# Content scores added to the positional scores tile by tile, and one product with the values

## The chip, the cores and the metric

The kernel runs on one core of one Trainium2 chip. The metric is device time in microseconds (us) of one execution; a figure for a kernel is the median of several executions.

## The reference, cut to what matters

Two layers work on an input of 4 images with 16 x 16 pixels and 1024 channels. Layer 0 is a convolution-like attention (a "lambda" layer), layer 1 is a causal attention with a mixture of eight experts behind it. Only layer 0 is touched. After a group norm it computes:

```
q = bn(x @ Wq);  k = x @ Wk;  v = bn(x @ Wv)       # 4 heads of q, one k, one v
q = q.reshape(b, heads, dim_v, m)                  # m = 256 pixels, dim 256
k = softmax(k.reshape(b, 1, dim_v, m), axis=-1)
v = v.reshape(b, 1, dim_v, m)
Lc = einsum('bukm,buvm->bkv', k, v)                # content
Yc = einsum('bhkn,bkv->bnhv', q, Lc)
rel = rel_pos_emb[rel_pos[..., 0], rel_pos[..., 1]]
Lp = einsum('nmku,buvm->bnkv', rel, v)             # position
Yp = einsum('bhkn,bnkv->bnhv', q, Lp)
x = x + (Yc + Yp).reshape(b, hh, ww, heads * dim_v)
```

Both terms end in a sum over m of a score with v: the content score is the sum over k of q and the softmax of k, the positional score is the sum over k of q and rel. The two kernels differ in whether the two scores are summed before the product with v. The reshapes are plain reinterpretations of memory, so a row of the matrix k after the reshape is made of pixels that lie 4 apart in x.

## The kernel before

Everything is float32. TensorE (PE) multiplies a stationary operand of up to 128 x 128 (loaded by LDWEIGHTS) with a moving operand of up to 512 columns; the results land in PSUM banks of 128 x 512. One pool of PSUM tiles has three banks tagged `mm` and three tagged `tr`, used in turn. A scheduler orders the instructions of each engine when the program is built; each engine then works through its own list strictly in order, and waits on semaphores. `small`, `l0`, `proj`, `tpool` and so on are pools in the on-chip memory SBUF. `big` has two places of 32 KB per partition, and `wpool` two of 16 KB; a new tile in such a place waits for the last use of the old one.

Layer 0 goes through these stages:

1. **Group norm and q.** `xn` (place `big0`) holds the normed input, channels on partitions. Products `pq` (L265) give q; VectorE (DVE) scales and shifts it (L269, L273) into `q0`, laid out [k within a half, half, pixel row i, pixel column j, batch and head]. The last index has 16 values, `BH`: four batches with four heads.
2. **k.** For each of eight tiles `t` (two for each batch) `pk` (L311) is a product over 8 chunks of channels with 256 result columns. VectorE takes the row maximum (L315), ScalarE (ACT) the exponential (L318), VectorE divides (L320). Two transposes `pkt` (L323) on TensorE and a copy (L324) put the result into `k_T`.
3. **v.** Four products `pv` (L334) and ScalarE's copies make `v_T`, pixels of m on partitions.
4. **Position.** In four rounds over `R` (in the order 1, 2, 0, 3), with 16, 15, 8 and 7 pixel rows `n_i`, GpSimd (POOL) copies a window of the embedding (L384), 32 products `pT` (L386) multiply it with q0, and ScalarE and VectorE take turns to copy the PSUM bank into `T` (L394). `T` is a tile of pool `tpool`, which has two of them. Then SyncE (SP) issues one or two transfers for each pixel row (L401), from `T` to its shifted place in `s0`, the positional scores [m within a half, half, i, j, BH] in place `big0`. R = 0 writes only upper pixel rows (ni from 8 on) of the first half of m; R = 3 writes only rows below 8, of the second half of m; R = 1 and R = 2 write both.
5. **Content.** `content()` is called before R = 3: four pairs of products `pl` (L355) of k_T and v_T make `lc` (ScalarE's copy, L362), which is Lc of the reference.
6. **First loop over the tiles.** For each of eight token tiles (batch b, half nt of the pixel rows) `pyc` (L414) multiplies q0 with lc; VectorE adds the result to `xs[t]`, the residual x (L421).
7. **Second loop.** For each tile `pyp` (L434) multiplies s0 with v_T; VectorE adds it to xs[t] (L441); `layer_norm` takes statistics (L159, L161), ScalarE normalises (L166), TensorE transposes (L170), ScalarE copies into `ln1` (L171) in place `big1`, where q0 was. GpSimd adds a bias to xs[t] (L443) and SP stores the row tile (L444).

After that `project_v` (products at L482) begins layer 1. It reads ln1, the first half of the tokens (tiles 0 to 3) first. Attention and the experts follow; they are the same in both kernels.

Of the kernel before, what the change touches and what calls it, by code (L numbers as in the profile page):

```python
# [30 lines left out]
F32 = mybir.dt.float32  # L31
I32 = mybir.dt.int32
AF = mybir.ActivationFunctionType
ALU = mybir.AluOpType
# [3 lines left out]
P = 128  # L38
C = 1024
NC = C // P  # L40
B = 4
M = 256
TOK = B * M
NT = TOK // P
HEADS0 = 4
BH = B * HEADS0
SIDE = 16
# [6 lines left out]
HALF = 512  # L54
# [9 lines left out]
def kernel(  # L64
# [27 lines left out]
    nc = tc.nc  # L92
# [13 lines left out]
    def big_tile(n, name, shape=(NC, TOK)):  # L106
        return big[n].tile([P, *shape], F32, tag="big", name=name)
# [11 lines left out]
    def mm(name):  # L119
        return ps.tile([P, HALF], F32, tag="mm", name=name)  # L120

    def tr(name):
        return ps.tile([P, HALF], F32, tag="tr", name=name)
# [7 lines left out]
    ident = const.tile([P, P], F32, tag="ident", name="ident")  # L131
# [7 lines left out]
    xs = tiles_of_x("x")  # L139
# [34 lines left out]
    with ExitStack() as layer0:  # L174
        l0 = pool(layer0, "l0")
        xn = big_tile(0, "xn")
# [8 lines left out]
            nc.gpsimd.dma_start(vp[:, i, :], a)  # L185
        emb = l0.tile([P, 2, REL, REL], F32, tag="emb", name="emb")
        v_T = l0.tile([P, 2, TOK], F32, tag="v_T", name="v_T")
        lc = l0.tile([P, B, 2, M], F32, tag="lc", name="lc")

        q0 = big_tile(1, "q0", (2, SIDE, SIDE, BH))  # L190

        with ExitStack() as projection:
            proj, projw = pool(projection, "proj"), pool(projection, "projw", 2)
# [5 lines left out]
            first_root = small.tile([P, 1], F32, tag="first_root", name="first_root", bufs=1)  # L199
            nc.scalar.activation(first_root, ident[:, 0:1], AF.Sqrt)  # L200

            q_scale = proj.tile([P, C], F32, tag="q_scale", name="q_scale")
            q_shift = proj.tile([P, C], F32, tag="q_shift", name="q_shift")
            bn = proj.tile([P, 2, C], F32, tag="bn", name="bn")
            mean_q, var_q = bn[:, 0, :], bn[:, 1, :]
            for t, a in ((q_scale, q_gamma), (q_shift, q_beta), (mean_q, q_mean), (var_q, q_var)):
                nc.sync.dma_start(t, a.partition_broadcast(P))
            nc.sync.dma_start(emb.rearrange("p c i j -> p c (i j)"), embT)
# [95 lines left out]
            w_kv = w_tile("w_kv", Wk, Wv)  # L304


            k_T = l0.tile([P, 2, B, 4, 64], F32, tag="k_T", name="k_T")
            for t in range(NT):
                pk = mm(f"pk{t}")
                for c in range(NC):  # L310
                    nc.tensor.matmul(  # L311
                        pk[:, :M], xn[:, c, ts(t, P)], w_kv[:, c, :M], start=(c == 0), stop=(c == NC - 1)
                    )
                top = small.tile([P, 1], F32, tag="k_top", name=f"k_top{t}")
                nc.vector.tensor_reduce(top, pk[:, :M], AX.X, ALU.max, negate=True)  # L315
                k_e = projw.tile([P, M], F32, tag="k_e", name=f"k_e{t}")
                total = small.tile([P, 1], F32, tag="k_total", name=f"k_total{t}")
                nc.scalar.activation(k_e, pk[:, :M], AF.Exp, bias=top, accum_out=total)  # L318
                nc.vector.reciprocal(total, total)
                nc.vector.tensor_scalar(k_e, k_e, total, None, ALU.mult)  # L320
                pt = tr(f"pkt{t}")
                for j in range(2):
                    nc.tensor.transpose(pt[:, ts(j, P)], k_e[:, ts(j, P)], ident)  # L323
                nc.vector.tensor_copy(  # L324
                    k_T[:, :, t // 2, :, ts(t % 2, 32)],
                    pt[:, : 2 * P].rearrange("p (j d k) -> p j k d", j=2, k=4),
                )


            for j in range(2):  # L330
                for th in range(2):
                    pv = mm(f"pv{j}_{th}")
                    for c in range(NC):
# [4 lines left out]
                            start=(c == 0),  # L338
                            stop=(c == NC - 1),
# [6 lines left out]
                        scale=vp[:, 0, j : j + 1],  # L346
                    )


        def content():  # L350
            for b in range(B):
                pl = mm(f"pl{b}")
                for kc in range(2):
                    for j in range(2):
                        nc.tensor.matmul(  # L355
                            pl[:, ts(kc, M)],
                            k_T[:, j, b, 2 * kc : 2 * kc + 2, :].rearrange("p k d -> p (k d)"),
                            v_T[:, j, ts(b, M)],
                            start=(j == 0),
                            stop=(j == 1),  # L360
                        )
                nc.scalar.copy(lc[:, b, :, :].rearrange("p k v -> p (k v)"), pl)  # L362

# [1 line left out]
        S2 = SIDE // 2  # L367
        s0 = big_tile(0, "s0", (2, SIDE, SIDE, BH))
        tpool = pool(layer0, "tpool", 2)
        for R, first, n_i in ((1, 0, 16), (2, 0, 15), (0, 8, 8), (3, 0, 7)):  # L370
            if R == 3:
                content()
            rows = min(S2, REL - S2 * R)
            parts = rows * SIDE
            group = 2 if n_i > S2 else 4
            T = tpool.tile([P, n_i, SIDE, BH], F32, tag="T", name=f"T{R}", padded_shape=[P, SIDE, SIDE, BH])
            for n0 in range(0, SIDE, group):
                pT = mm(f"pT{R}_{n0}")
                out_T = pT[:parts, : group * BH * n_i].rearrange("p (j i h) -> p j i h", j=group, h=BH)
                for g in range(group):  # L380
                    nj = n0 + g
                    at = SIDE - 1 - nj
                    window = tpool.tile([P, 2, rows, SIDE], F32, tag="window", name=f"window{R}_{nj}", bufs=4, padded_shape=[P, 2, S2, SIDE])
                    nc.gpsimd.tensor_copy(window, emb[:, :, S2 * R : S2 * R + rows, at : at + SIDE])  # L384
                    for kc in range(2):
                        nc.tensor.matmul(  # L386
                            out_T[:, g, :, :],
                            window[:, kc, :, :].rearrange("p i j -> p (i j)"),
                            q0[:, kc, first : first + n_i, nj, :],
                            start=(kc == 0),  # L390
                            stop=(kc == 1),
                        )
                evict = nc.scalar.copy if n0 // group % 2 == 0 else nc.vector.tensor_copy
                evict(T[:parts, :, n0 : n0 + group, :].rearrange("p i j h -> p j i h"), out_T)  # L394
            for i in range(n_i):
                ni = first + i
                start = S2 * R + ni - SIDE + 1
                for mh in range(2):
                    lo, hi = max(start, mh * S2), min(start + rows, mh * S2 + S2)
                    if lo < hi:  # L400
                        nc.sync.dma_start(  # L401
                            s0[(lo - mh * S2) * SIDE : (hi - mh * S2) * SIDE, mh, ni, :, :],
                            T[(lo - start) * SIDE : (hi - start) * SIDE, i, :, :],
                        )


        for t in range(NT):
            b, nt = divmod(t, 2)
            for hp in range(2):
                py = mm(f"pyc{t}_{hp}")  # L410
                for hl in range(2):
                    bh = b * HEADS0 + 2 * hp + hl
                    for kc in range(2):
                        nc.tensor.matmul(  # L414
                            py[:, ts(hl, M)],
                            q0[:, kc, ts(nt, S2), :, bh].rearrange("p i j -> p (i j)"),
                            lc[:, b, kc, :],
                            start=(kc == 0),
                            stop=(kc == 1),
                        )  # L420
                nc.vector.tensor_add(xs[t][:, ts(hp, HALF)], xs[t][:, ts(hp, HALF)], py)  # L421

        ln1 = big_tile(1, "ln1")
        ln_rows = wpool.tile([P, 4, C], F32, tag="w", name="ln_rows")
        bp = ln_rows[:, 3, :]
        nc.gpsimd.dma_start(bp, b_proj.partition_broadcast(P))
        for t in range(NT):
            b, nt = divmod(t, 2)
            for hp in range(2):
                py = mm(f"pyp{t}_{hp}")  # L430
                for hl in range(2):
                    bh = b * HEADS0 + 2 * hp + hl
                    for mh in range(2):
                        nc.tensor.matmul(  # L434
                            py[:, ts(hl, M)],
                            s0[:, mh, ts(nt, S2), :, bh].rearrange("p i j -> p (i j)"),
                            v_T[:, mh, ts(b, M)],
                            start=(mh == 0),
                            stop=(mh == 1),
                        )  # L440
                nc.vector.tensor_add(xs[t][:, ts(hp, HALF)], xs[t][:, ts(hp, HALF)], py)  # L441
            layer_norm(ln_rows[:, t % 3, :], t, ln1)
            nc.gpsimd.tensor_add(xs[t], xs[t], bp)  # L443
            nc.sync.dma_start(x_rows[ts(t, P), :], xs[t])  # L444
    x_home.close()
# [788 lines left out]
```

## Time and profile before

| | us |
|---|---|
| median of 3 runs | 1333.54 (1332.22 to 1333.65) |
| the profiled execution | 1332.32 |
| its span, first to last instruction | 1330.5 |
| TensorE busy in the span | 1289.7 |
| VectorE busy | 664.7 |
| GpSimd busy | 348.9 |
| ScalarE busy | 247.6 |
| mean granted TensorE clock | 0.992 of full speed |

The times in all views count from the first instruction. PE stands for matmuls, PEld for LDWEIGHTS, which overlap them. One float32 matmul instruction appears as two rows. A timeline line gives the start, the length, the engine, the line of the code, the operation, output<-input, the shape and the count; a bracket tells how long the engine was idle before it and what ended that. "SPq" are transfers that SyncE issues. A line of stretches gives its borders, its length, the busy time of PE, PEld, DVE, ACT and POOL, and then the granted clock, the share of the DMA engines and GB/s. The part of the trace that the change touches runs from about 129 us (`pk`) to 302 us (the first `project_v`).

### The profile page before, as it was taken

How to read it: one execution, taken by the hardware profiler on the slowest of the kernel's cores; microseconds unless marked ns; L12 is line 12 of the kernel's file. 1: busy time of each engine (PE TensorE's matmuls, PEld its weight loads, DVE VectorE, ACT ScalarE, POOL GpSimd, SP SyncE). 2: the span in 40 equal slices, each digit the busy share in tenths (PEclk: the TensorE clock that was granted, in tenths of full speed). 3: DMA queues.
4: the chain of work that ended last, by engine and by line, in shares of the span. 5: the costliest groups of instructions: out<-in, count | busy, mean ns of one | idle time of the engine just before them, and what ended most of it. 6: DMA issues, size and time to landing. Idle time of an engine off the chain costs nothing. (4 is left out here: it accounts for less than half of the span.)

```text
span 1330.5 us, 12205 instructions
## 1 busy us (share of the span) xinstructions
PE 1289.7 (97%) x4492; PEld 710.3 (53%) x4492; DVE 664.7 (50%) x1255; ACT 247.6 (19%) x577; POOL 348.9 (26%) x370
## 2 busy tenths in 40 slices
PE   6999999999999999999999998999999999999994
PEld 3444759998884555555554544444444444444442
DVE  5664301377232555554444756664645555554641
ACT  3200111041000333333323322111101111011110
POOL 0000015042000111112111113545444535445520
PEclk9999999999999999999999999999999999999997
DMA  9210013113102202010505215375666557474532
GB/s 355 117 64 16 0 64 95 34 80 112 64 1 64 64 0 64 1 64 1 190 15 194 95 64 204 91 210 132 184 162 155 160 140 203 101 233 93 114 62 33
DMA packets 60944, 136.11 MB, mean 102 GB/s; under 512 B 5936, under 2 KB 20288, under 8 KB 60880
## 3 DMA queue, kind: packets, MB, share of 16 engines
q1 hardware_dynamic: 47232, 93.27, 20.2%
q0 software_dynamic: 13648, 42.01, 14.5%
q8 instruction: 37, 0.61, 0.2%
q14 instruction: 27, 0.22, 0.1%
HBM read 97.51 MB, written 33.55 MB: 99 GB/s over the span
## 5 line engine op out<-in xcount | busy, mean ns | idle before, releaser
L708 POOL DMA_INDIRECT w_e_xg<-rows,gather x156 | 163.4, 1047 | 69.1 <-issue 44.5
L1078 PE MATMUL p<-w_e,A 128*128 128x512 f32 x384 | 171.8, 597 | 1.8 <-DVE slot L945 1.8
L598 POOL TENSOR_TENSOR s<-s,total 128x256 f32<-128x256 f32 x64 | 51.5, 826 | 341.2 <-DVE total L595 341.2
L1078 PEld LDWEIGHTS p<-w_e,A 128*128 128x128 f32 x384 | 73.5, 191 | 94.1 <-issue 92.4
L639 PE MATMUL po<-w_p,y_T 128*128 128x512 f32 x256 | 116.1, 598 | 0.0
L736 POOL DMA_INDIRECT out_dram<-y,add x32 | 58.6, 1832 | 214.3 <-ACT y L1084 146.5
L1078 PE MATMUL p<-T,S 128*128 128x512 f32 x256 | 112.7, 592 | 0.0
L1084 ACT ACTIVATE y<-y,slot 128x512 f32<-128x512 f32 x64 | 46.2, 722 | 340.1 <-DVE y L1092 166.8
L265 PE MATMUL pq<-w_q,xn 128*128 128x512 f32 x224 | 101.0, 603 | 1.6 <-ACT xn L244 1.6
L729 PE MATMUL one_pe<-w_e,one 128*128 128x512 f32 x224 | 97.3, 592 | 0.0
L482 PE MATMUL pqk<-ln,w_qk 128*128 128x512 f32 x192 | 85.0, 592 | 0.0
L1078 PEld LDWEIGHTS p<-T,S 128*128 128x128 f32 x256 | 48.6, 190 | 60.8 <-issue 60.7
L639 PEld LDWEIGHTS po<-w_p,y_T 128*128 128x128 f32 x256 | 46.3, 190 | 49.1 <-issue 48.7
L729 PEld LDWEIGHTS one_pe<-w_e,one 128*128 128x128 f32 x224 | 42.6, 190 | 53.6 <-issue 53.6
L265 PEld LDWEIGHTS pq<-w_q,xn 128*128 128x128 f32 x224 | 42.5, 193 | 51.8 <-issue 48.6
L588 ACT ACTIVATE s<-s,top 128x256 f32<-128x256 f32 (+1 forms) x128 | 56.6, 443 | 17.4 <-DVE top L586 17.3
L482 PEld LDWEIGHTS pqk<-ln,w_qk 128*128 128x128 f32 x192 | 35.9, 190 | 42.1 <-issue 41.1
L718 DVE STREAM_TRANSPOSE A<-w_e_xg 128x1024 f32<-128x1024 f32 x32 | 39.7, 1240 | 36.1 <-DMA w_e_xg<-rows,gather 36.1
L482 PE MATMUL pqk<-T,S_qk 128*128 128x512 f32 x128 | 57.7, 593 | 0.0
L1078 PE MATMUL p<-w_e,S 128*128 128x512 f32 x128 | 57.5, 592 | 0.0
L1078 PE MATMUL p<-T,A 128*128 128x512 f32 x128 | 57.5, 592 | 0.0
L611 ACT COPY s_T<-pst 128x384 f32<-128x384 f32 x64 | 27.5, 481 | 158.3 <-PE pst L610 158.3
(251 smaller groups left out, 1791.5 us busy)
## 6 DMA issues: line engine op xcount, KB each, us to landing
w_e<-in_expert_w_dram SPq DMA_DIRECT2D x16, 2048.0 KB
w_qk<-in_W_attnT_dram SPq DMA_DIRECT2D x8, 1024.0 KB
xn<-in_xT_dram SPq DMA_DIRECT2D x8, 512.0 KB
x<-in_x_dram SPq DMA_DIRECT2D x8, 512.0 KB
w_v<-in_W_attnT_dram SPq DMA_DIRECT2D x2, 2048.0 KB
x_rows<-x SPq DMA_DIRECT2D x8, 512.0 KB
w_p<-in_W_projT_dram SPq DMA_DIRECT2D x2, 2048.0 KB
xb<-x_rows SPq DMA_DIRECT2D x8, 512.0 KB
```

What stands on the lines that cost most here:

```text
L265: nc.tensor.matmul(pq, xn[:, c, ts(t, P)], w_q[kc][:, c, :], start=(c == 0), stop=(c == NC - 1))
L482: nc.tensor.matmul(bank, stationary(c), moving(c), start=(c == 0), stop=(c == NC // 2 - 1))
L588: nc.scalar.activation(s[:, h, cols], s[:, h, cols], AF.Exp, bias=top[:, qt, h : h + 1], accum_out=total[:, qt, h : h + 1],)
L598: nc.gpsimd.tensor_mul(s[:, :, cols], s[:, :, cols], total[:, qt, :].unsqueeze(2).to_broadcast([P, 2, (qt + 1) * P]),)
L611: nc.scalar.copy(s_T[:, h, :], pt[:, : 3 * P])
L639: nc.tensor.matmul(po, y_T[:, c, ts(t, P)], w_p[j][:, c, :], start=(c == 0), stop=(c == NC - 1))
L708: nc.gpsimd.indirect_dma_start(out=row[:, g, :], out_offset=None, in_=table[: (TOK - P) * Q, :] if e == 0 else table, in_offset=bass.Indir ...
L718: nc.vector.transpose(row_T.rearrange("p c (g j) -> p g c j", g=Q), row.rearrange("p g (c i) -> p g c i", c=NC),)
L729: nc.tensor.matmul(pe, row_T[:, c, :], w[j][:, c, :], start=(c == 0), stop=(c == NC - 1))
L736: nc.gpsimd.indirect_dma_start(out=out[: TOK - P, :] if e == 0 else out, out_offset=bass.IndirectOffsetOnAxis(ap=add[:, e, k : k + 1], axi ...
L1078: nc.tensor.matmul(bank, a[:, c, :], b[:, c, :], start=(c == 0), stop=(c == NC // 2 - 1))
L1084: nc.scalar.mul(y[i][:, ts(j, HALF)], y[i][:, ts(j, HALF)], slot[:, e, 1, 2 * pair + i : 2 * pair + i + 1])
```

## The change

The content scores are computed as scores, not through Lc, and added into s0 before the product with v. It has these parts:

- **k.** `k_q` takes the place of `k_T`: [k row within a half, batch, half, m]. `pk` is computed in two halves of 64 result rows for each chunk; the stationary operand is every fourth token of one batch. The softmax result goes straight into k_q; `pkt`, its copy and `k_T` go.
- **Content.** `content(b, ih)` is now called for each tile. For each half `mh` of m it multiplies k_q with q0 (two matmuls of 512 columns: 128 pixels of one half, 4 heads) and VectorE adds the bank into s0. `lc`, `pl`, the `lc` copies, and the first loop with `pyc` and its additions go.
- **Second loop.** The order of the tiles is all batches with the upper pixel rows (nt = 1), then all with the lower ones. content of the next tile is called ahead of the product `py` (before: `pyp`) of the present one.
- **Places.** q0 moves to pool `l0`; `q_scale`, `q_shift` and the batch norm rows move into a tile `q_rows` in place `big1`. The two T buffers become two halves of one tile `two_T`, also in `big1`, used in turn. `tpool` keeps only the windows. `ln1` takes its place in `big1` after two_T.

The diff, cut to its core:

```diff
-        lc = l0.tile([P, B, 2, M], F32, tag="lc", name="lc")
-        q0 = big_tile(1, "q0", (2, SIDE, SIDE, BH))
+        q0 = l0.tile([P, 2, SIDE, SIDE, BH], F32, tag="q0", name="q0")
...
-            q_scale = proj.tile([P, C], F32, tag="q_scale", name="q_scale")
...
+            q_rows = big_tile(1, "q_rows", (NC, TOK))
+            q_scale, q_shift, mean_q, var_q = (q_rows[:, i, :] for i in range(4))
...
-            k_T = l0.tile([P, 2, B, 4, 64], F32, tag="k_T", name="k_T")
+            k_q = l0.tile([P, B, 2, M], F32, tag="k_q", name="k_q")
             for t in range(NT):
+                b, kc = divmod(t, 2)
                 pk = mm(f"pk{t}")
                 for c in range(NC):
-                    nc.tensor.matmul(
-                        pk[:, :M], xn[:, c, ts(t, P)], w_kv[:, c, :M], start=(c == 0), stop=(c == NC - 1)
-                    )
+                    for kl in range(2):
+                        nc.tensor.matmul(
+                            pk[kl * 64 : kl * 64 + 64, :M],
+                            xn[:, c, ts(b, M)].rearrange("p (d r) -> p r d", r=4)[:, 2 * kc + kl, :],
+                            w_kv[:, c, :M],
+                            start=(c == 0),
+                            stop=(c == NC - 1),
+                        )
...
-                nc.vector.tensor_scalar(k_e, k_e, total, None, ALU.mult)
-                pt = tr(f"pkt{t}")
-                for j in range(2):
-                    nc.tensor.transpose(pt[:, ts(j, P)], k_e[:, ts(j, P)], ident)
-                nc.vector.tensor_copy(
...
+                nc.vector.tensor_scalar(k_q[:, b, kc, :], k_e, total, None, ALU.mult)
...
+        def content(b, ih):
+            heads = slice(b * HEADS0, b * HEADS0 + HEADS0)
+            for mh in range(2):
+                pc = (tr if mh else mm)(f"pc{ih}_{b}_{mh}")
                 for kc in range(2):
...
+                    nc.tensor.matmul(
+                        pc,
+                        k_q[:, b, kc, ts(mh, P)],
+                        q0[:, kc, ts(ih, S2), :, heads].rearrange("p i j h -> p (i j) h"),
+                        start=(kc == 0),
+                        stop=(kc == 1),
+                    )
+                to = s0[:, mh, ts(ih, S2), :, heads].rearrange("p i j h -> p (i j) h")
+                nc.vector.tensor_add(to, to, pc.rearrange("p (n h) -> p n h", h=HEADS0))
...
-        for R, first, n_i in ((1, 0, 16), (2, 0, 15), (0, 8, 8), (3, 0, 7)):
-            if R == 3:
-                content()
+        two_T = big_tile(1, "two_T", (2, SIDE, SIDE, BH))
+        for n, (R, first, n_i) in enumerate(((1, 0, 16), (2, 0, 15), (0, 8, 8), (3, 0, 7))):
...
-            T = tpool.tile([P, n_i, SIDE, BH], F32, tag="T", name=f"T{R}", padded_shape=[P, SIDE, SIDE, BH])
+            T = two_T[:, n % 2, :n_i, :, :]
...
-        for t in range(NT):
-            b, nt = divmod(t, 2)
-            for hp in range(2):
-                py = mm(f"pyc{t}_{hp}")
...
-                nc.vector.tensor_add(xs[t][:, ts(hp, HALF)], xs[t][:, ts(hp, HALF)], py)
...
-        for t in range(NT):
-            b, nt = divmod(t, 2)
+        tiles = [(b, nt) for nt in (1, 0) for b in range(B)]
+        for i, (b, nt) in enumerate(tiles):
+            if i == 0:
+                content(b, nt)
+            if i + 1 < NT:
+                content(*tiles[i + 1])
+            t = 2 * b + nt
...
-            layer_norm(ln_rows[:, t % 3, :], t, ln1)
+            layer_norm(ln_rows[:, i % 3, :], t, ln1)
```

More of the change, by code (lines that the diff above doesn't have):

```diff
@@ L200 @@
             nc.scalar.activation(first_root, ident[:, 0:1], AF.Sqrt)
-            q_scale = proj.tile([P, C], F32, tag="q_scale", name="q_scale")
-            q_shift = proj.tile([P, C], F32, tag="q_shift", name="q_shift")
-            bn = proj.tile([P, 2, C], F32, tag="bn", name="bn")
-            mean_q, var_q = bn[:, 0, :], bn[:, 1, :]
+            q_rows = big_tile(1, "q_rows", (NC, TOK))
+            q_scale, q_shift, mean_q, var_q = (q_rows[:, i, :] for i in range(4))
             for t, a in ((q_scale, q_gamma), (q_shift, q_beta), (mean_q, q_mean), (var_q, q_var)):
@@ L319 @@
                 nc.vector.reciprocal(total, total)
-                nc.vector.tensor_scalar(k_e, k_e, total, None, ALU.mult)
-                pt = tr(f"pkt{t}")
-                for j in range(2):
-                    nc.tensor.transpose(pt[:, ts(j, P)], k_e[:, ts(j, P)], ident)
-                nc.vector.tensor_copy(
-                    k_T[:, :, t // 2, :, ts(t % 2, 32)],
-                    pt[:, : 2 * P].rearrange("p (j d k) -> p j k d", j=2, k=4),
-                )
+                nc.vector.tensor_scalar(k_q[:, b, kc, :], k_e, total, None, ALU.mult)
             for j in range(2):
@@ L347 @@
                     )
-        def content():
-            for b in range(B):
-                pl = mm(f"pl{b}")
+        def content(b, ih):
+            heads = slice(b * HEADS0, b * HEADS0 + HEADS0)
+            for mh in range(2):
+                pc = (tr if mh else mm)(f"pc{ih}_{b}_{mh}")
                 for kc in range(2):
[L354 to L362, printed above, removed]
+                    nc.tensor.matmul(
[7 more added lines that the diff above has]
+                nc.vector.tensor_add(to, to, pc.rearrange("p (n h) -> p n h", h=HEADS0))
         S2 = SIDE // 2
@@ L404 @@
                         )
-        for t in range(NT):
-            b, nt = divmod(t, 2)
-            for hp in range(2):
-                py = mm(f"pyc{t}_{hp}")
[L411 to L421, printed above, removed]
         ln1 = big_tile(1, "ln1")
@@ L426 @@
         nc.gpsimd.dma_start(bp, b_proj.partition_broadcast(P))
-        for t in range(NT):
-            b, nt = divmod(t, 2)
+        tiles = [(b, nt) for nt in (1, 0) for b in range(B)]
[5 more added lines that the diff above has]
+            t = 2 * b + nt
             for hp in range(2):
-                py = mm(f"pyp{t}_{hp}")
+                py = mm(f"py{t}_{hp}")
                 for hl in range(2):
```

## The prediction

> **What bounds the kernel.** I read the page's busy times first, then the groups by line of the first 400 us, then the timeline of the stretch that the change touches.
>
> ```profile
> PE 1289.7 (97%) x4492; PEld 710.3 (53%) x4492; DVE 664.7 (50%) x1255; ACT 247.6 (19%) x577; POOL 348.9 (26%) x370
> ```
>
> TensorE has work in 97% of the span, so a microsecond counts if it leaves TensorE's queue, or makes that queue wait. The groups (busy us, mean ns; a float32 matmul shows as two rows, called passes here):
>
> ```profile
> L334 PE MATMUL pv<-xn,w_kv 128*128 128x512 f32 x64 | 27.8, 592 | 0.0
> L311 PE MATMUL pk<-w_kv,xn 128*128 128x256 f32 x128 | 28.9, 379 | 0.0
> L311 PEld LDWEIGHTS pk<-w_kv,xn 128*128 128x128 f32 x128 | 23.8, 190 | 3.4 <-issue 0.5
> L323 PE MATMUL pkt<-ident,k_e 128*128 128x128 f32 x16 | 3.3, 288 | 0.3
> L355 PE MATMUL pl<-v_T,k_T 128*128 128x256 f32 x32 | 7.1, 379 | 0.0
> L414 PE MATMUL pyc<-lc,q 128*128 128x256 f32 x128 | 28.8, 387 | 0.0
> L414 PEld LDWEIGHTS pyc<-lc,q 128*128 128x128 f32 x128 | 28.5, 307 | 0.0
> L421 DVE TENSOR_TENSOR x<-x,pyc 128x512 f32<-128x512 f32 x16 | 11.0, 687 | 17.7 <-PE pyc L414 17.7
> ```
>
> Busy time over count is the pace: 27.8/64 = 0.434 us for a pass of 512 columns, 0.226 for 256. Passes overlap, so means are longer than paces. The last column is idle time of the engine before the group: VectorE waits for TensorE here, not the reverse. Around the scores:
>
> ```profile
> 202.31 40.14 SPq L401 DMA_DIRECT2D s<-T  x60
> 219.25 1.20 ACT L394 COPY T<-pT 128x512 f32<-128x512 f32 x2 [5.80 <-DMA s<-T]
> 219.98 2.02 PE L386 MATMUL pT<-q,window 128*128 128x128 f32 x16 [0.15 <-POOL window L384]
> 221.84 7.07 PE L355 MATMUL pl<-v_T,k_T 128*128 128x256 f32 x32
> 228.75 4.88 PE L386 MATMUL pT<-q,window 128*112 128x112 f32 x48
> 234.34 0.97 ACT L394 COPY T<-pT 112x448 f32<-112x448 f32 x2 [4.80 <-DMA s<-T]
> 235.01 1.80 PE L386 MATMUL pT<-q,window 128*112 128x112 f32 x16 [1.38 <-ACT T L394]
> ```
>
> The second pacemaker is SP: 60 transfers from T to s0 go out one by one, 40.14/60 = 0.669 us each: 23 for R=1, 22 for R=2, 8 for R=0, 7 for R=3 (counted from the loop). Copies into a reused T buffer wait for them (bracket: 5.80 and 4.80 us); TensorE shows only 1.38 us of it, because `pl` and three free PSUM banks cover the rest.
>
> **What the Trainium skill says.** (1) "TensorE: Matmul & The Clock Gate", section "Part 3: Packing small matmuls": results that go to different column groups are computed at the same time. The trace agrees, on attention values with halves of 64 columns:
>
> ```profile
> 507.56 0.87 PE L620 MATMUL pa<-s_T,v 128*64 128x256 f32 x8
> 508.36 0.92 PE L566 MATMUL sc<-qk 64*128 64x256 f32 x8
> ```
>
> Eight passes, four of 256 and four of 128 columns, would take 4 x 0.226 + 4 x 0.113 = 1.36 us in a row; the next group starts after 0.80. (2) "SBUF — State Buffer", section "Door 1: The DMA port swizzle", on 16-byte lines: at least two accesses per line are needed for full rate. The trace agrees on weight loads: `pyc` loads every sixteenth float in 28.5/128 = 0.223 us, 1.74 ns per column, where the mean of a dense load is 190 ns and of this one 307. A moving operand in 16-byte pieces is not in this trace. (3) The first page again, "Part 1: The HAM clock gate": a window of about 3.4 us with TensorE mostly idle is followed by half clock. The trace agrees:
>
> ```profile
> 806.90 1.07 PE L809 MATMUL row_pt<-ident,row 128*128 128x128 f32 x8 [3.68 <-DVE row L827]
> 808.00:812.00 4.00, 3.90 (x22) 1.47 (x23) 3.04 (x12) 0.37 (x1) 0.00 (x0) 0.57 1.05 409
> ```
>
> After a wait of 3.68 us the clock (third number from the end) is 0.57; the wait of 1.38 us at 235 did no such thing.
>
> **Part by part.** Times are on the clock of the trace before until the sum.
>
> *k stage.* The transposes `pkt` go: -3.3 us. The `pk` matmuls double to 128 instructions with 64 result rows each; by (1) a pair runs in the time of one, so 28.9 us stays. Their weights are every fourth float, one per 16-byte line: 64 x 1.74 ns = 0.111 us, free if the two halves load together, and 0.223 per pair against 0.216 to 0.226 of streaming if not: 0 to +1, I take +0.6. Net -2.7. The copies to k_T (3.4 us) leave VectorE, which idles for TensorE there (7.9 before `pk`'s reduction): nothing.
>
> *Content.* `pl` goes: -7.1; `pyc` goes: -28.8. Instead 32 matmuls with 512 columns, 64 passes, moving q0 in pieces of four floats. Four accesses per line should keep the full pace: 64 x 0.434 = 27.8. Bounds: 27.8, and 64 x 512 x 1.74 ns = 57.0 if each float cost what it costs in a strided load; a gain below 27.8 is excluded, dense 512-column passes being no quicker. I take 27.8.
>
> *T halves.* T is now one region in big1, and a copy waits only for transfers that read the pixel rows it overwrites. The copy of R=0 (8 rows) waits for the first 8 of R=1's 23 transfers: 219.25 - 15 x 0.669 = 209.2, before its matmuls end. TensorE's 0.15 goes, and R=0 ends at 221.7. R=3's first three groups follow at once: 226.6. The fourth needs the bank of the first, whose copy (7 rows) waits for 14 of R=2's 22 transfers: 234.34 - 8 x 0.669 = 229.0, plus 0.49 of copy: 229.5. So with `pl` gone TensorE stands 2.9 us instead of 1.4. Fourth group: 231.3.
>
> *First tiles.* Content of the first two tiles, 16 passes, takes 6.9: 238.2. Then `py` of the first waits for two adds into s0, and the second of these for R=0's eight transfers, which follow R=2's: 234.34 + 8 x 0.669 = 239.7, plus 0.69 for the add (from L421's row): 240.4. TensorE stands 2.2 us. Queued behind that add on VectorE are the adds of the second tile, needed later. R=3's seven land at about 244.4; the lower rows and the first write of ln1 over two_T need them only some 10 us and more after 240.
>
> *Second loop.* Before, it ran from `pyp`'s start at 265.24 to `project_v` at 301.90, 36.7 us. It now also holds 48 passes of content, 20.8 us. On VectorE each tile gets two adds of 0.69 in place of L421's; with some 7.9 us per tile for about 5.1 us of its work they fit, yet they stand in one queue with the layer norm. In the built order a tile's transposes come about as much TensorE work after its last product as its norm takes, so small waits appear: I add 0.5 (bounds 0 and 8 x 0.7 = 5.6, one add late per tile). One more set of transposes falls behind the loop's end, which changes its place and not the sum. So 240.4 + 36.7 + 20.8 + 0.5 = 298.4 against 301.9: -3.5.
>
> *Costed at nothing.* ScalarE loses four `lc` copies (2.3 us), waits for TensorE. The windows take freed space and can start after the last q0 add near 133; needed at 187. q0, q_scale and the rest change address only. The eight x_rows stores keep their number on SP, behind the same POOL adds; the rows return after 690. If that cover went, half a microsecond each.
>
> *Clock.* Two waits of 2.9 and 2.2 us, 9 us apart, lie between 1.38 (no throttle) and 3.68 (throttle). Half clock for 3.4 us loses 1.7; the first loss falls into the second wait. For the second +0.6 (bounds 0 and 1.7).
>
> **Sum.** -2.7 - 3.5 + 0.6 = -5.6 us. The profiled execution took 1332.32 (span 1330.5 and 1.8 around it), so 1326.7 for it; it lies 1.2 below the median of the three runs shown, so the median goes to **1327.9**. A check by work alone: 3.3 + 7.1 + 28.8 - 27.8 - 0.6 = 10.8 us leave TensorE, and 3.6 + 0.5 + 0.6 come back as waits and clock: -6.1.
>
> **Rivals.**
> *Slow moving operand (8%).* If pieces of 16 bytes stream as badly as single floats load, a pass takes 512 x 1.74 ns = 0.89 us. That is 64 x 0.457 = 29.2 more, of which 2.2 fall into the wait for R=0: 1354.9, slower. For it: the strided loads' 307 ns. Against: four accesses per line, where the loads have one. It decides from x = (5.6 + 2.2)/64 = 0.12 us more per pass, a pace of 0.556.
> *Halves in a row (4%).* If `pk`'s halves do not overlap, 128 pairs cost 0.216 more each, 27.6: 1355.5. Against: the `pa` rows.
> *VectorE sets the tile's pace (14%).* A norm held up by 0.7 us per tile, eight times, in place of my 0.5: +5.1, 1333.0, no change. For it: VectorE works two thirds of the time there. Against: L421 idled for TensorE.
> *T is still released whole (3%).* Then R=3's copy stays at 234.34, content ends at 235.0 + 1.8 + 6.9 = 243.7 and `py` starts there: +3.3, 1331.2. Against: the waits of the built program.
>
> **From cases to numbers.** My forecast has 69%, and 2% are for what I have not seen: the forecast's own range, from the unknown load, clock and norm costs, is 1323.5 to 1331. With the 17% of the two milder rivals at 1331 to 1333.5, 1323.5 to 1333.5 leaves out somewhat under 2 in 10. A change of 0.2%, 2.7 us, is about what a measurement of this kernel can tell from none. Faster by more: 0.71, nearly all of the forecast (0.66) and a part of the milder rivals (0.05); within: 0.15; slower: 0.14, the two slow cases and the unseen.
>
> **What would show it.** Right: `pk` near 29 us with 256 passes, `pkt`, `pl`, `pyc` gone; content at 0.43 per pass; one TensorE wait of 2 to 3 us before R=3's last group, one before the first `py`; `project_v` about 6 us earlier. Wrong: content passes over 0.5, `pk` at 56, LDWEIGHTS of `pk` over 0.2, waits before the transposes of each tile, clock below 0.9 after 225.

## The result, and the profile after

The changed kernel takes 1327.37 us (median of 6 executions, 1326.66 to 1329.55) against 1333.6 of the kernel before in the same comparison (1332.22 to 1336.36). The ratio is 0.9955, with a 95% interval from 0.9943 to 0.9968: 6.0 us faster, where 5.6 was forecast. The profiled execution of the changed kernel is the slowest of its six: 1329.55, with a span of 1327.7.

First the busy times, from the head of the page:

```profile
PE 1281.9 (97%) x4508; PEld 691.1 (52%) x4508; DVE 659.8 (50%) x1247; ACT 245.4 (18%) x573; POOL 348.1 (26%) x370
```

TensorE's busy time fell by 7.8 us, and its share of the span is the same. The groups of the first 400 us (busy us, mean ns, idle time before) show what was exchanged for what:

```profile
L310 PE MATMUL pk<-w_kv,xn 128*64 128x256 f32 x256 | 27.9, 380 | 0.0
L310 PEld LDWEIGHTS pk<-w_kv,xn 128*64 128x64 f32 x256 | 25.5, 193 | 2.8 <-issue 0.8
L351 PE MATMUL pc<-q,k_q 128*128 128x512 f32 x64 | 29.6, 593 | 0.0
L420 PE MATMUL py<-v_T,s 128*128 128x256 f32 x128 | 31.8, 400 | 3.0 <-DMA s<-two_T 3.0
L359 DVE TENSOR_TENSOR s<-s,pc 128x512 f32<-128x512 f32 x16 | 10.8, 684 | 18.7 <-PE pc L351 13.9 <-DMA s<-two_T 4.9
L170 PE MATMUL ln_pt<-ident,ln_rows 128*128 128x128 f32 x64 | 8.5, 276 | 1.4 <-ACT ln_rows L166 1.4
```

The rows `pkt`, `pl` and `pyc` are gone. `pk` has twice the passes in 27.9 us. A pass of content starts every 0.43 us; the 29.6 is larger than 64 x 0.43 because the passes are spread over many short groups, and the last pass of each counts with its full 0.59 us. The last row has one wait only: the transposes of seven tiles found their input ready, those of the last tile waited 1.4 us.

The timeline around the scores (start, length, engine, and in brackets the idle time ahead with what ended it):

```profile
211.91 28.72 SPq L397 DMA_DIRECT2D s<-two_T  x43
226.48 0.97 ACT L390 COPY two_T<-pT 112x448 f32<-112x448 f32 x2 [8.37 <-DMA s<-two_T]
227.15 1.80 PE L382 MATMUL pT<-q,window 128*112 128x112 f32 x16 [3.21 <-ACT two_T L390]
228.79 7.04 PE L351 MATMUL pc<-q,k_q 128*128 128x512 f32 x16
238.03 1.88 DVE L359 TENSOR_TENSOR s<-s,pc 128x512 f32<-128x512 f32 x3 [4.86 <-DMA s<-two_T]
238.82 5.46 PE L420 MATMUL py<-v_T,s 128*128 128x256 f32 x16 [2.99 <-DMA s<-two_T]
```

Both forecast waits are there. The copies of R=3 start at 226.48, when the fourteenth transfer of R=2 has landed; TensorE stood 3.21 us for the bank that they free. Then `py` stood 2.99 us, for the add at 238.03, which stood for the transfers of R=0. `py` took 5.46 us for 16 passes in place of some 3.7. The clock says why (third number from the end, in stretches of 4 us):

```profile
234.00:238.00 4.00, 1.83 (x5) 0.52 (x3) 0.00 (x0) 0.00 (x0) 0.00 (x0) 1.00 0.52 151
238.00:242.00 4.00, 3.18 (x8) 2.56 (x9) 1.88 (x3) 0.00 (x0) 0.00 (x0) 0.61 0.33 87
242.00:246.00 4.00, 4.00 (x15) 3.05 (x14) 2.97 (x5) 0.00 (x0) 0.00 (x0) 0.96 0.00 0
```

After the second wait TensorE ran at half clock for about 3.4 us, which lost up to 1.7.

### The profile page after: what moved, and what is told of

It is laid out like the page before. It is cut to its first block, busy times and chain, and to the rows that moved or that the text cites. A ratio compares the mean times of both kernels' runs of the same rounds, so it can differ in the third digit from the quotient of the medians.

```text
span 1327.7 us, 12229 instructions
## 1 busy us (share of the span) xinstructions
PE 1281.9 (97%) x4508; PEld 691.1 (52%) x4508; DVE 659.8 (50%) x1247; ACT 245.4 (18%) x573; POOL 348.1 (26%) x370
## 5 line engine op out<-in xcount | busy, mean ns | idle before, releaser
L715 PEld LDWEIGHTS one_pe<-w_e,one 128*128 128x128 f32 x224 | 42.6, 190 | 53.5 <-issue 53.3
```

Of the source, the lines that this page charges most:

```text
L715: nc.tensor.matmul(pe, row_T[:, c, :], w[j][:, c, :], start=(c == 0), stop=(c == NC - 1))
```

## The experiments

Unless another base is named, each is an edit of the changed kernel. Ratios are to the kernel before, run on the same chip; 0.001 is 1.33 us.

### Two queues for the transfers

```
-evict = nc.scalar.copy if n0 // group % 2 == 0 else nc.vector.tensor_copy
+evict = nc.vector.tensor_copy
-nc.sync.dma_start(
+(nc.scalar if i % 2 else nc.sync).dma_start(
```

> The changed kernel, but the transfers from two_T to s0 go out in turn from SP's queue and from ScalarE's, 30 each, and VectorE makes all the copies into two_T, so that ScalarE's queue holds only transfers there. Theory (the pace of one issuing queue sets both waits of TensorE): the transfers end near 200 + 30 x 0.64 = 219 us instead of 240, the waits of 3.21 us before R=3's last group and of 2.99 us before the first py go, and with them the half clock after the second, worth up to 1.7: -6.2 to -7.9 on 1327.4, so 1319.5 to 1321.2. Rival 1 (the transfers themselves are slow, not their issue): both waits stay, 1327.4. Rival 2 (TensorE's next wait takes over: the 12 more copies on VectorE, or the layer norm's transposes): a part of the gain only, 1323 to 1326.

1321.93 us, ratio 0.9909 (0.9893 to 0.9924): some 5.4 to 6.1 below the changed kernel (by medians, by ratios), a little less than the 6.2 to 7.9 expected. The timeline of this run:

```profile
200.28 28.41 ACTq L397 DMA_DIRECT2D s<-two_T  x28
200.31 28.72 SPq L397 DMA_DIRECT2D s<-two_T  x32
225.75 7.04 PE L351 MATMUL pc<-q,k_q 128*128 128x512 f32 x16
232.63 3.72 PE L420 MATMUL py<-v_T,s 128*128 128x256 f32 x16
```

No bracket is left on TensorE's lines, and the 16 passes of `py` take 3.72 us: no wait, no half clock. Issue on one queue set both waits. In the changed kernel's trace each transfer holds SP for 0.59 us, the next follows at 0.64, and a transfer lands about 2 us after its issue, so that three are under way at once: what goes one by one is the issue. Whether SP itself takes the 0.59 us or is held by the queue behind it, the trace does not tell. Two numbers of the expectation were wrong: the transfers end at 229, not 219, and the queues issue 28 and 32, not 30 each. Each queue needs about 0.65 us for a transfer, but both now run dry between the rounds of R and wait for the next copies. The pacemaker has moved to TensorE. This is the fastest kernel of the study.

### Its control: only VectorE copies

The first of the two edits above alone.

> The changed kernel with all copies into two_T on VectorE and the transfers still on SP alone: the control for two_queues, which makes both edits. Theory (issue on one queue is what two_queues mended): both waits of TensorE stay, 1327.4, within 0.8. Rival (ScalarE's copies were the trouble): 1321 to 1323 as in two_queues.

1328.25 us, ratio 0.9965 (0.9952 to 0.9978). Both waits stay:

```profile
227.94 3.17 PE L382 MATMUL pT<-q,window 128*112 128x112 f32 x16 [3.10 <-DVE two_T L390]
238.77 3.91 PE L420 MATMUL py<-v_T,s 128*128 128x256 f32 x16 [0.78 <-DMA s<-two_T]
```

The time is 0.9 above the changed kernel, a little outside the 0.8 expected; no gain came from the copies. The second wait is short here because the half clock came after the first wait: the group of R=3 took 3.17 us in place of 1.80, time that TensorE would otherwise have stood. In most of the runs below half clock came behind the first wait too, and in pk_dense, more_vector and lower_first it lasted 6.8 us there. So 3.4 us of half clock cost up to 1.7 when they fall after the second wait, and next to nothing when they fall before it.

### The same two edits in the kernel before

> The kernel before, with the transfers from T to s0 going out in turn from SP's queue and from ScalarE's, and all copies into T on VectorE: the same edit as in two_queues. Theory (the kernel before loses only 1.4 us to SP's pace, since pl's products and free banks cover the rest): its waits of 1.38 and 0.15 us go, ratio to the kernel before 0.9988, and two_queues, with the work of the change and no wait for transfers in either, then lies the full 10.8 us of removed TensorE work below it. Rival (SP's pace costs the kernel before as much as the changed one): ratio 0.995 and a distance of only 5 to 6 us.

1332.99 us, ratio 0.9993 (0.9983 to 1.0004), no difference that can be told. Its waits of 1.38 and 0.15 us went, but another came, because `lc`'s copies on ScalarE now stand in a queue with transfers:

```profile
227.43 1.99 PE L355 MATMUL pl<-v_T,k_T 128*128 128x256 f32 x8 [0.85 <-ACT lc L362]
```

The distance to two_queues is 0.0084, or 11.2 us, which the two intervals leave open by some 2.5 either way: the removed TensorE work in full (by work alone the prediction had 10.8). With transfers on one queue the distance is 6.0, so about half of the removed work came back as waits and half clock.

### Halves of two_T given back whole

```
 T = two_T[:, n % 2, :n_i, :, :]
+if n > 1:
+    last = two_T[:, n % 2, 17 - n, 0, :]
+    nc.scalar.copy(last[:, 0:1], ident[:, 0:1])
+    nc.vector.tensor_copy(last[:, 1:2], ident[:, 0:1])
```

> The changed kernel, but the halves of two_T are given back whole: ahead of the copies of R=0 and R=3, ScalarE and VectorE each write one float per partition into the last pixel row of the half (not read afterwards), which the last transfer of the older R reads. Theory (row-wise release is part of the gain): R=3's last group waits for all 22 transfers of R=2 instead of 14, 8 x 0.64 = 5.1 us later, 232.3; content then ends at 241.2 and py starts there instead of at 238.8: +2.4, and up to +1.7 more if the longer wait brings half clock for longer: 1329.8 to 1331.5. Rival (only the wait for R=0's transfers before py counts, R=3's wait is inside it): no change, 1327.4.

1326.39 us, ratio 0.9953 (0.9938 to 0.9967): no change. For R=3 this tested nothing: in the built order the two writes stand behind three of the four copies. For R=0 the copies did wait for the last transfer of R=1:

```profile
216.40 0.19 ACT L375 COPY two_T<-ident 128x1 f32<-128x1 f32 x1 [6.29 <-DMA s<-two_T]
217.46 6.74 PE L386 MATMUL pT<-q,window 128*128 128x128 f32 x64 [0.97 <-ACT two_T L394]
226.21 2.06 PE L386 MATMUL pT<-q,window 128*112 128x112 f32 x16 [2.00 <-ACT two_T L394]
```

The new wait of 0.97 us before R=0's matmuls is repaid at once: R=3's last group waits 2.00 instead of 3.21 and starts 42.44 us after the first `pT`, exactly as in the changed kernel (42.43). SP's pace sets that start, and what TensorE does in between doesn't move it. (Here and below the first `pT` is the start of its first weight load, 0.4 us ahead of its first pass.)

### The same, forced by position

```
-T = two_T[:, n % 2, :n_i, :, :]
+T = two_T[:, n % 2, n // 2 * 8 : n // 2 * 8 + n_i, :, :]
```

> The changed kernel, with R=0 in pixel rows 8 to 15 of its half of two_T and R=3 in rows 8 to 14, in place of the first rows, so that their copies wait for the last transfer of the older R: all 23 of R=1, all 22 of R=2. (The run t_whole did not force that for R=3: three of the four copies were placed ahead of the write that waits.) In the built order of this kernel three pairs of content's passes stand ahead of R=3's last group. Theory (whole release is made up by products that need no copy): R=3's copy ends near 232.2, its group 1.6 us later, ten passes of content fill the time to 238.1, and py waits for R=0's transfers as in the changed kernel: 1327.4, within 0.8. Rival (the prediction's fourth rival: the wait comes on top): +2.4 to +3.3, 1329.8 to 1330.7.

1327.5 us, ratio 0.9964 (0.9953 to 0.9976). TensorE:

```profile
223.97 2.75 PE L351 MATMUL pc<-q,k_q 128*128 128x512 f32 x6
231.97 3.30 PE L382 MATMUL pT<-q,window 128*112 128x112 f32 x16 [5.25 <-ACT two_T L390]
235.06 4.52 PE L351 MATMUL pc<-q,k_q 128*128 128x512 f32 x10
239.42 3.71 PE L420 MATMUL py<-v_T,s 128*128 128x256 f32 x16
```

The wait for all 22 transfers is 5.25 us, but six passes of content went ahead of it, the other ten fill the time behind it, and `py` starts 55.1 us after the first `pT`, against 54.1. The prediction's fourth rival took 3.3 us for whole release; it costs 0 to 1.2. Releasing T by rows was not where the gain came from.

### Lower pixel rows first

```
-tiles = [(b, nt) for nt in (1, 0) for b in range(B)]
+tiles = [(b, nt) for nt in (0, 1) for b in range(B)]
```

> The changed kernel with the lower pixel rows (nt=0) of all batches first, then the upper ones. Theory: the first tile then needs R=3's seven transfers, the last of 60: issued at 240.0, landed near 242.5, the add done near 243.3, py there instead of at 238.8: +4.5, with up to +1.7 for half clock: 1331.9 to 1333.6. Rival (the order of rows doesn't matter, since the layer norm or other TensorE work fills the wait): 1327.4.

1331.81 us, ratio 0.9983 (0.9975 to 0.9991): 3.7 to 4.4 us slower than the changed kernel, at the edge of the expectation.

```profile
243.20 1.28 DVE L359 TENSOR_TENSOR s<-s,pc 128x512 f32<-128x512 f32 x2 [4.58 <-DMA s<-two_T]
243.94 4.66 PE L420 MATMUL py<-v_T,s 128*128 128x256 f32 x12 [2.58 <-DVE s L359]
```

Counted from the first `pT`, the twelve passes of `py` that wait for R=3's transfers start 58.1 us in, against 54.1. Four others ran first, which the expectation did not have. The twelve take 4.66 us, at half clock, as those of the changed kernel do.

### pk: dense weights, and halves in a row

pk_dense takes 128 matmuls with 128 dense columns, as before; pk_row has the loop over `kl` outside that over `c`.

> The changed kernel with pk computed as before: 128 instructions with dense 128-column weights, result rows in pixel order, so that k_q holds the pixels in another order than the scores need (that part of the computation is changed). Theory (the two 64-row halves overlap fully and the strided loads hide behind the matmuls): the pk stage stays at 28 us and the time at 1327.4, within 0.7. Rival (strided loads or the doubled number of instructions cost something in the stage): 0.6 to 1 us of it goes, 1326.4 to 1326.8.

> The changed kernel with the two 64-row halves of each pk tile one after the other (all eight chunks of the first half, then all eight of the second) in place of alternating. Theory (alternating halves run at the same time): only at the border of two halves do passes overlap now, so the 256 passes take nearly 0.216 us each, 27 us more in the pk stage: 1354, and pk's busy time near 55. Rival (64-row results are quicker by themselves, whatever their order): 1327.4.

pk_dense: 1326.4 us, ratio 0.994 (0.9927 to 0.9954), which is 1.0 to 2.0 us below the changed kernel, with intervals that overlap: more than the 0.7 of the theory, and the rival's number. The trace tells the two apart better:

```profile
130.57 27.79 PE L309 MATMUL pk<-w_kv,xn 128*128 128x256 f32 x128
185.67 38.80 PE L377 MATMUL pT<-q,window 128*128 128x256 f32 x240
```

From the first pass of `pk` to the first of `pT` it takes 55.10 us, the changed kernel 55.41 (129.73 to 185.14, shown further down). So the halves with their strided loads cost about 0.3 us, less than the rival had, and not nothing. Within the stage a pair of half passes starts every 0.216 us, as a dense pass does; the 0.3 lies at the stage's ends.

pk_row: 1343.14 us, ratio 1.0071 (1.0051 to 1.0092). From the first pass of `pk` to that of `pv` it takes 44.26 us, the changed kernel 27.84. The groups, pk_dense first:

```profile
L309 PE MATMUL pk<-w_kv,xn 128*128 128x256 f32 x128 | 27.8, 379 | 0.0
```

```profile
L310 PE MATMUL pk<-w_kv,xn 128*64 128x256 f32 x256 | 44.3, 386 | 0.0
```

Alternating halves run at the same time. In a row they cost 16.4 us more, not 27: in the trace 90 of the 255 distances between starts are below 0.15 us, six at each of the 15 borders between halves, where the others are 0.216. At each border this saves 0.75 us, the time of three to four passes: that many of the next half run beside the last ones of this half. That is argued from the distances; the depth was not varied.

### A moving operand of single floats

```
-q0[:, kc, ts(ih, S2), :, heads].rearrange("p i j h -> p (i j) h")
+q0[:, :, :, :, 4 * b + 2 * ih + kc].rearrange("p c i j -> p (c i j)")
```

> The changed kernel with content's moving operand taken as 512 single floats 64 bytes apart (one head-column of q0 over both of its halves) in place of 128 pieces of four floats; the content scores are therefore other numbers. It prices the rival of a slow moving operand. If a float moved alone costs the 1.74 ns of a strided weight load, a pass takes 0.89 us, 64 x 0.457 = 29.2 us more, of which about 3 fall into the wait before py: 1353. If the stride of a moving operand has no price at all, 1327.4, and a piece of four floats could have had none.

1351.74 us, ratio 1.0147 (1.0132 to 1.0161).

```profile
L351 PE MATMUL pc<-q,k_q 128*128 128x512 f32 x64 | 57.0, 1031 | 0.0
```

A pass starts every 0.858 us, so a float alone costs 0.858 / 512 = 1.68 ns when it is moved as well. By work, 64 x (0.858 - 0.43) = 27.4 us more, less the wait of 3.0 before `py` that it fills and the 1.7 of half clock that no longer follows: 22.7. Measured were 24.4 by medians and 25.6 by ratios; the four executions lie between 1349.84 and 1353.91, so some 2 us stay open. The prediction's first rival had a true price; pieces of four floats escape it.

### More work on VectorE

```
 nc.vector.tensor_add(to, to, pc.rearrange("p (n h) -> p n h", h=HEADS0))
+nc.vector.tensor_scalar(to, to, 1.0, None, ALU.mult)
```

> The changed kernel with one more VectorE pass over the same 512 elements per partition after each of the 16 adds of content into s0 (times 1.0). Theory (VectorE has slack in the second loop): some 0.4 to 0.7 us of VectorE each, 6 to 11 us in all, of which only the one ahead of the first py and perhaps a little before transposes is seen: +0.4 to +1.5, 1327.8 to 1328.9. Rival (the prediction's third: VectorE sets the pace of a tile): the whole 6 to 11 us, 1333 to 1338.

1328.23 us, ratio 0.996 (0.9946 to 0.9973): 0.7 to 0.9 more, inside the expectation of the slack.

```profile
L359 DVE TENSOR_TENSOR s<-s,pc 128x512 f32<-128x512 f32 x16 | 10.9, 681 | 12.1 <-PE pc L351 10.1 <-DMA s<-two_T 1.9
L360 DVE TENSOR_SCALAR s<-s 128x512 f32<-128x512 f32 x16 | 9.7, 613 | 0.3
```

9.7 us more work on VectorE, and under one on the path. VectorE doesn't set a tile's pace.

### An attempt to go on: weight sums on GpSimd

```
-def sums_of_A(a11, a12, a21, a22, s1, s2, s4):   # four nc.vector operations
+def sums_of_A(a11, a12, a21, a22, s1, s2, s4, eng=nc.vector):   # the same on eng
-    sums_of_A(*a, s1, s2, s4)
+    sums_of_A(*a, s1, s2, s4, nc.vector if r else nc.gpsimd)   # in project_v
```

> two_queues, and the four weight sums ahead of the first quarter of project_v on GpSimd instead of VectorE. In the traces the last tile's layer norm stands on VectorE behind the first of these sums (1.2 and 2.8 us), and TensorE waits 1.37 us for its transposes. Theory (that queue is the cause): the wait of 1.37 goes, the time lies 1 to 1.4 us below two_queues, ratio to the kernel before near 0.990. Rival (GpSimd takes 2.4 us for each sum and the products of the sums wait for it): no gain, or 1 to 3 us slower than two_queues.

1326.13 us, ratio 0.9946 (0.9929 to 0.9963): 4.2 to 4.9 us slower than two_queues. The wait before the last transposes fell from 1.38 to 0.54 us, so that queue was the cause of most of it. But a larger one came:

```profile
L457 DVE TENSOR_TENSOR T<-ln,T 128x2048 f32<-128x2048 f32 x1 | 4.1, 4104 | 0.0
```

```profile
L150 POOL TENSOR_TENSOR s_v<-w_v 128x1024 f32<-128x1024 f32 x1 | 2.4, 2367 | 0.0
L152 POOL TENSOR_TENSOR s_v<-w_v,s_v 128x1024 f32<-128x1024 f32 x1 | 4.4, 4402 | 0.0
```

```profile
308.67 3.78 PE L468 MATMUL pv<-w_v,ln 128*128 128x256 f32 x8 [4.27 <-POOL w_v L153]
```

A sum takes GpSimd 2.37 us alone and 4.40 beside VectorE's sums over ln1, and these rise with it, from 2.28 in two_queues (the same line there) to 4.10. The two engines hold each other up, and TensorE waits 4.27 us for the last sum. The Trainium skill ("SBUF — State Buffer", "SBUF: two separate sides") says so: one pair of ports serves both, and a GpSimd operation or a VectorE operation with two inputs in SBUF holds it for the whole instruction. The durations agree: each becomes nearly the sum of the two, 2.37 + 2.28 = 4.65. Behind the wait of 4.27 us half clock lasts 6.8 us, which no other run has at this place; it loses up to 3.4 more.

## Why the prediction was right

Its mechanism and its sum held. The stages, each against the kernel before in the two profiled executions, in us, from first pass to first pass; the predicted column puts its steps together in the same way:

| stretch | predicted | measured |
|---|---|---|
| span's start to first `pk` | 0 | +0.7 (129.73 against 129.00) |
| first `pk` to first `pT` | -2.7 | -3.1 (55.41 against 58.54) |
| first `pT` to the second loop's first product (`py`; before `pyp`) | -24.8 | -24.0 (53.68 against 77.70) |
| from there to the end of `project_v`'s wait for T | +21.9 | +20.9 (74.40 against 53.46) |
| sum | -5.6 | -5.5 |

The lines behind it, the kernel before first (`py` of the changed kernel, at 238.82, is shown above):

```profile
129.00 6.64 PE L311 MATMUL pk<-w_kv,xn 128*128 128x256 f32 x30
187.54 32.29 PE L386 MATMUL pT<-q,window 128*128 128x256 f32 x176
265.24 9.52 PE L434 MATMUL pyp<-v_T,s 128*128 128x256 f32 x42
318.70 2.86 PE L482 MATMUL pv<-s_v,T 128*128 128x256 f32 x12 [0.99 <-DVE T L471]
```

```profile
129.73 27.91 PE L310 MATMUL pk<-w_kv,xn 128*64 128x256 f32 x256
185.14 38.80 PE L382 MATMUL pT<-q,window 128*128 128x256 f32 x240
313.22 2.86 PE L468 MATMUL pv<-s_v,T 128*128 128x256 f32 x12 [0.99 <-DVE T L457]
```

That the sums agree to 0.1 is luck: four misses of 0.4 to 1.0 cancel. The first, +0.7, is hardly the change's: q's first product starts at 13.52 us here and at 12.87 in the trace before, and anywhere from 12.3 to 13.7 in the thirteen traces.

Beyond the last of these stretches the two profiled executions differ for another reason. Behind the waits of 3.7 and 1.8 us before the experts the half clock lasted 6.8 us each in the changed kernel's records, and 3.4 each in the kernel before. That is 3.4 us lost in code that is the same in both, and the main reason why the profiled spans differ by 2.8 only. The medians, over more executions, give 6.0 to 6.2. They are not free of it either: the mean granted clock is 0.989 over the six executions of the changed kernel and 0.992 over the sixty of the kernel before in the later comparisons. The difference, 0.0024 unrounded, is 3.2 us of a span, and the half clock behind `py` explains 1.7. Why the rest is lost stays open.

*k stage.* The transposes went, and the halves overlap. With pk_dense between the two kernels the terms come apart: the transposes were worth 3.4 us (58.54 to 55.10), forecast 3.3, and the halves with their strided loads cost 0.3 (55.10 to 55.41), for which +0.6 was taken.

*Content.* 64 passes at 0.43 us: the lower bound held. The rival's price of single floats, 1.74 ns from the weight loads, was close to the 1.68 measured in pc_single for single floats that are moved.

*T halves.* R=3's last group was put 42.4 us after the first `pT` (229.5 less 187.11, its weight load in the trace before) and started after 42.4; the wait of TensorE is 3.2, forecast 2.9. R=0's copies no longer hold TensorE.

*First tiles.* `py` was put 53.3 us after the first `pT` and started after 54.1. The term that failed is the time of 16 transfers, 16 x 0.669 = 10.7: from the copy at 226.48 to the add at 238.03 it was 11.55. In the trace one transfer of this stretch held SP for 1.66 us where the others took 0.59. So the wait is 3.0 instead of 2.2.

*Second loop.* The +0.5 for transposes that come too early was not needed: none of the first seven tiles waited. The kernel before had two such waits, which the forecast carried over in its 36.7 us and which are gone:

```profile
278.42 1.09 PE L170 MATMUL ln_pt<-ident,ln_rows 128*128 128x128 f32 x8 [0.34 <-ACT ln_rows L166]
296.36 1.09 PE L170 MATMUL ln_pt<-ident,ln_rows 128*128 128x128 f32 x8 [0.39 <-ACT ln_rows L166]
```

But the last tile's transposes wait 1.37 instead of 0.74, because VectorE, by the order of its queue, does weight sums of `project_v` between that tile's statistics and the rest of its norm. The forecast did not have this; by luck it is 0.6 for the 0.5 that it had elsewhere.

*Clock.* +0.6 between 0 and 1.7: in the profiled execution it was the upper end, in dve_evict nearly nothing. "The first loss falls into the second wait" is what dve_evict shows. The Trainium skill ("TensorE: Matmul & The Clock Gate", "Part 1: The HAM clock gate") says that the window runs freely, whenever the kernel starts, so that a stretch falls where the window happens to end. The traces agree: in each of the thirteen, the starts of half clock and its ends inside the kernel lie whole multiples of 3.413 us apart (in the changed kernel it starts at 238.89, 802.09 and 843.05). Windows laid out on this grid show why nearly the same waits end differently. In the changed kernel a border cuts the first wait, so that TensorE stands 1.3 us of one window and 1.9 of the next, and full clock goes on; 3.0 us of the second wait lie in one window, and half clock follows. In dve_evict 2.6 us of the first wait lie in one window. Around the scores, in all traces, half clock followed every full-clock window in which TensorE stood for 2.0 us or more, and none with 1.9 or less. So waits well below 3.4 us are enough, and the phase of the window decides; the phase itself was not varied.

*Rivals.* VectorE's pace, slow moving pieces and halves in a row were each tried and are not what happens. Whole release was given 3.3 us and costs 0 to 1.2, because products that need no copy fill the wait; in that rival the step that failed is the unchanged order of TensorE's queue.

## What to carry to other kernels

When work leaves the bounding engine, ask which queue it had been covering: here half of 11 us came back as waits for transfers that one queue issued at 0.64 us each, and a second issuing queue freed them. Two waits on the same pacemaker are one wait: making the first longer or shorter moved nothing here, only the pacemaker's last item counted. A strided operand is priced by its pieces, and pieces of four floats were enough here.

## What was not expected of the hardware

- A half clock stretch beside two neighbouring waits cost from nearly nothing to 1.7 us, by where it fell (3.17 us for R=3's group in dve_evict, 5.46 for `py` in the changed kernel), and 2.0 us of standing inside one window of 3.413 us were enough for it.
- Passes with results in different column groups overlap without alternating, three to four at each border: 44.26 us where 256 x 0.216 = 55.3 would be in a row.
- GpSimd and VectorE slow each other by 1.8 to 1.9 in float32 sums out of SBUF (2.37 to 4.40 us, 2.28 to 4.10).
- ScalarE's queue issued transfers beside SP's at 0.65 us each, where SP alone took 0.64.
